# Row maxima recorded a step earlier in a two-layer attention kernel planned at build time

## The chip, the cores and the metric

The kernel runs on one core of one Trainium2 chip. The metric is the device time of one execution in microseconds (us), here 1409.2 us as the median of three runs (1408.99 to 1411.39). The profile is of one more execution, which took 1410.37 us.

## What is computed

Two conditioned attention layers over x of shape (8, 512, 512). The first is a linear attention with a softmax over the features of q and one over the tokens of k. The second, in which the change lies, is an ordinary softmax attention with 16 heads of 32 features in each of 8 batches:

```python
xn = layer_norm(x, norm_w, norm_b)
q = (xn @ q_w + q_b).reshape(Bx, Tx, H, -1)
k = (xn @ k_w + k_b).reshape(Bx, Tx, H, -1)
att = jnp.einsum('bnhl,bmhl->bnmh', q, k)
att = att + (1.0 - mask) * -1000000.0
att = jax.nn.softmax(att, axis=2)
v = ((xn @ v_w + v_b) * src_mask[:, :, None]).reshape(Bx, Tx, H, -1)
y = jnp.einsum('bnmh,bmhl->bnhl', att, v).reshape(Bx, Tx, Dx)
...
h = layer_norm(y, sb_norm_w, sb_norm_b) * (1.0 + scale) + shift
h = jax.nn.silu(h) @ out_w + out_b
return x + h
```

The softmax runs over the 512 keys of each query and head. Any number subtracted from all scores of one query and head drops out of it.

## The kernel before

**Recording and planning.** The kernel doesn't issue instructions as it is read. Every call (`nc.tensor.matmul`, `nc.sync.dma_start` and so on) is recorded by `Order`, with the tiles that it reads and writes; what depends on what follows from the order of recording (`touch`): a read that is recorded after a write waits for it, and a read recorded before a write makes that write wait. `Order.place` then makes a plan, twelve times over: an estimated duration for every instruction (`_takes`), an estimated time for every DMA (`DMA_ISSUE`, `DMA_LAND`, `DMA_RATE`), a list of what is ready for each engine, and of that the instruction with the earliest latest start (`slack`). The best of the twelve plans is issued, and each engine then runs its list strictly in that order. All instructions therefore carry line 476 in the profile, and are told apart by their tiles.

**The second layer** works in 32 groups G (8 batches b, 4 groups of 4 heads each, G = 4b + g). A group has two stacked operands in SBUF, `qst[G % 3]` and `kst[G % 3]`, of 106 rows, so three groups' stacks are alive at a time. Rows 0 to 97 hold q and k in two parts, and the mask. Rows 98 to 105 of `qst` hold the negated maximum of each query and head, in two parts; the same rows of `kst` select it, so that the product of all 106 rows is the score less that maximum.

- `l1_max(G)`: 16 products of 98 rows (queries on the partitions, 4 chunks by 4 heads), each followed by a maximum along the row on VectorE into `nm`. Then the maxima are split into `mi`, transposed by four small matmuls, copied to `aux` (tag `z`) on ScalarE, and a DMA on SyncE's queue spreads them into rows 98 to 105 of `qst` (lines 1089 to 1099).
- `l1_att(G)`: 16 products of 106 rows (keys on the partitions, key chunk m by head j), each followed by an exponential on ScalarE into a tile `e` (tag `A`), and after each key chunk `l1_av`, which multiplies by v and adds the exponentials up on GpSimd or VectorE.
- `l1_qk(G)`, `l1_stack(G)`: the projections of q and k, written out to DRAM and gathered from there into the stacks by six DMAs of 256 KB.
- `values`, `l1_y`, `l1_tail`, `transpose_x`: v, and the layer's output, interleaved by `pump` from a table of costs and due steps.

**The order of recording around the change.** `l1_max` and `l1_att` are generators. The loop at line 1422 records one of the 16 steps of `l1_att(G)` and then takes `next(maxes)` once, where `maxes` chains `l1_max(1)` to `l1_max(31)`; four `next` calls (`LEAD`) are made ahead of the loop, and in batch 7 group 28 makes eight more (lines 1424 to 1426). `l1_max(G)` has 15 yields between its 16 products, one ahead of `mi` (line 1088), and one at its end: 17 calls a group, of a loop that makes 16. So the `mi` part of group G is recorded in call 17 G, while the first score of group G is recorded after 4 + 16 G calls. Up to group 4 the maxima come first. From group 5 on the first G - 4 scores of a group are recorded ahead of the group's own maxima, and read the rows that the stack's previous user, group G - 3, left there; from group 20 on all 16 do. The loop makes 4 + 16 x 32 + 8 = 524 calls of the 527 that groups 1 to 31 ask for, so group 31 records 14 of its 16 maxima and no `mi` part.

Of the kernel before, what the change touches and what calls it, by code (L numbers as in the profile page):

```python
# [521 lines left out]
def kernel(ctx: ExitStack, tc: tile.TileContext, x, cond, mask0, mask1, w0, w1, out):  # L522
# [16 lines left out]
    def big(tag, name, dtype=F32, shape=(P, 512)):  # L539
        t = sb.tile(list(shape), dtype, name=name, tag=tag, bufs=BUFS[tag])  # L540
        if tag == "stk":
            nc.gpsimd.memset(t[:, :, 0:1].bitcast(F32), 0.0)
        return t

    def bank(tag, name, parts=P):
        tag = {"S": "mm", "ST": "mm", "a": "mm"}.get(tag, tag)
        return ps.tile([parts, 512], F32, name=name, tag=tag, bufs=BANKS[tag])
# [4 lines left out]
    def chunk(i):  # L552
        return slice(i * P, (i + 1) * P)
# [258 lines left out]
    st = {}  # L812
# [265 lines left out]
    def l1_max(G):  # L1078
        q, k = qst[G % 3], kst[G % 3]
        nm = sm.tile([P, NC, 4], F32, name=f"nm{G}", tag="nm4")  # L1080
        for c in range(NC):
            for j in range(4):
                if c or j:
                    yield
                sp = bank("S", f"s{G}{c}{j}")
                nc.tensor.matmul(sp, q[0:98, j, chunk(c)], k[0:98, j, :], start=True, stop=True)
                nc.vector.tensor_reduce(nm[:, c, j : j + 1], sp, AX.X, ALU.max, negate=True)
        yield
        mi = sm.tile([P, NC, 2, 4], F32R, name=f"mi{G}", tag="mi")
        nc.vector.tensor_copy(mi[:, :, 0, :], nm)  # L1090
        nc.vector.tensor_tensor(mi[:, :, 1, :], nm, mi[:, :, 0, :].bitcast(F32), ALU.subtract)
        mp = bank("S", f"mp{G}", 8)
        for c in range(NC):
            nc.tensor.transpose(mp[:, chunk(c)], mi[:, c].bitcast(F32).rearrange("p t j -> p (t j)"), ident)
        aux = big("z", f"aux{G}", shape=(8, 512))
        nc.scalar.copy(aux.bitcast(F32R), mp)
        nc.sync.dma_start(
            q[98:106].bitcast(F32), aux.unsqueeze(1).broadcast_to([8, 4, 512])
        )
        yield  # L1100

    SPARE = {(2, 2): "bWq", (2, 3): "bWk"}

    def l1_att(G):
        b, g = divmod(G, 4)
        q, k = qst[G % 3], kst[G % 3]
        if g == 0:
            st["yT", b] = []
        st["yp", G] = bank("a", f"yT{G}")
        st["acc", G] = []  # L1110
        for m in range(NC):
            cur = []
            for j in range(4):
                sp = bank("ST", f"t{G}{m}{j}")
                nc.tensor.matmul(sp, k[:, j, chunk(m)], q[:, j, :], start=True, stop=True)
                e = big(SPARE.get((m, j), "A"), f"e{G}{m}{j}")
                nc.scalar.activation(e, sp, AF.Exp)
                cur.append(e)
                if j == 1 and m > 0:
                    l1_av(G, m - 1)  # L1120
                yield
            st["e", G, m] = cur

    def l1_av(G, m):
        b, g = divmod(G, 4)
        while len(st["L1", "v", b]) <= m:
            st["need"]()
        es, yp = st.pop(("e", G, m)), st["yp", G]
        with order.together(845.0 if m or not G else 1690.0):
            if m == 0 and G > 0:  # L1130
                den = l1_den(G - 1)
            for j in range(4):
                h = 4 * g + j
                nc.tensor.matmul(
                    yp[32 * j : 32 * j + 32, :],
                    st["L1", "v", b][m][:, 32 * h : 32 * h + 32],
                    es[j],
                    start=(m == 0),
                    stop=(m == NC - 1),
                )  # L1140
        if m == 0 and G > 0:
            l1_den_keep(G - 1, den)
        acc = st["acc", G]
        if m == 0:
            acc.extend(es)
        else:
            for j in range(4):
                with order.on("gpsimd", "vector"):
                    nc.gpsimd.tensor_tensor(acc[j], acc[j], es[j], ALU.add)
        if m == NC - 1:  # L1150
            t = big("yT", f"yTs{G}")
            nc.scalar.copy(t, st.pop(("yp", G)))
            st["yT", b].append(t)
# [122 lines left out]
    for b in range(B + 1):  # L1276
# [5 lines left out]
        if b == 0:  # L1282
            bias_wide("L0", "Wv")
            run(first)
            split_w("L0", "Wv")
            bias_wide("L0", "Wq")
            split_w("L0", "Wq")
            prep_cond()
            with order.after(*st["L0", "xs", 1]):
                load_emb("L0", nc.sync)  # L1290
            l1_cols = load_cols("L1", list(COLS), nc.sync)
            run(second)
            run(l0_kn(b))
            split_w("L0", "Wo")
            load_bo("L0")
        else:
            run(mix(l0_y(b - 1), first, 4, 6))
            if last:
                l1_init(0)
                l1_stack(0)  # L1300
            run(islice(second, 26 if not last else 24))
            run(mix(hidden("L0", b - 1, "S"), second, 4, 7))
            tail = output("L0", b - 1, x[b - 1], x1[b - 1])
            if not last:
                run(mix(l0_kn(b), tail, 4, 12))
            else:
                load_x("L1", 1, x1[1])
                tail = mix(values("L1", 0), tail, 13, 12)
                run(mix(l1_max(0), tail, 1, 6))
# [56 lines left out]
    def ahead(b):  # L1366
# [5 lines left out]
        if n < B:  # L1372
# [5 lines left out]
            for g in range(3 if n else 4):  # L1378
                yield from l1_qk(4 * n + g)

    maxes = chain.from_iterable(l1_max(G) for G in range(1, NG))
    for _ in range(LEAD):
        next(maxes)
# [3 lines left out]
    for b in range(B):  # L1387
# [30 lines left out]
        for g in range(4):  # L1418
            G = 4 * b + g
            if G > 0:  # L1420
                l1_av(G - 1, NC - 1)
            for i, _ in enumerate(l1_att(G)):
                next(maxes, None)
                if b == B - 1 and g == 0 and i % 4 == 0:
                    for _ in range(2):
                        next(maxes, None)
                if i == STK and 0 < G < NG - 2:
                    while ("d", "Wq", G + 2) not in st:
                        need()
                    l1_stack(G + 2)  # L1430
                pump(16 * g + i)
# [60 lines left out]
```

## Time and profile before

| What | Value |
|---|---|
| Median of three runs | 1409.2 us |
| The profiled execution | 1410.37 us |
| Its span, first to last instruction | 1408.6 us |
| Mean granted TensorE clock | 0.992 |
| VectorE row maxima of the second layer | 510, mean 683 ns |
| Products of 98 rows | 510, mean 422 ns |
| Products of 106 rows | 512, mean 420 ns |
| DMAs `qst<-z` that spread the maxima | 31, 64 KB each |
| Idle time of PE in front of a matmul, by what ended it, ending with `DMA qst<-z` | 3.8 us, 2 times |

The page gives busy time by engine and by group of instructions. [...]matmuls overlap, and follow each other at about 235 ns in a run of products of 512 columns. An engine's name with a q is its queue. In a row of the waits, the engine and tile that waited stand left of the arrow, what ended the wait right of it, then the sum, the number and the longest. The chain of waits is the chain of work that ended last.

### The profile page before, as it was taken

The numbers are of one execution on the slowest core, as the hardware profiler recorded it, in microseconds if no ns is written. First come the engines' busy times: TensorE is split into PE (matmuls) and PEld (weight loads), VectorE is DVE, ScalarE is ACT, GpSimd is POOL, SyncE is SP. The second block draws the span as 40 slices with busy tenths as digits, with TensorE's granted clock in tenths as the row PEclk, the third lists the DMA queues.
The fourth block names the chain that finished last, engine by engine and source line by source line (L and its number), as shares of the span: only waits on it lengthen the run. The fifth ranks groups of instructions, "written<-read, shape, count | busy, mean of one in ns | idle before, by whom it ended". The sixth has DMA issues, their size and how long they took to land.

```text
span 1408.6 us, 20819 instructions
## 1 busy us (share of the span) xinstructions
PE 1370.6 (97%) x7385; PEld 956.9 (68%) x7385; DVE 1034.9 (73%) x1804; ACT 703.6 (50%) x1330; POOL 635.7 (45%) x721
## 2 busy tenths in 40 slices
PE   7999999999999998998999999999999999999996
PEld 4788878888888687556566566566666566666554
DVE  7665575666656568886878878778878777787987
ACT  4242323333234343654755655754854764764772
POOL 5123415133241312756537446555436546545661
PEclk9999999999999999999999999999999999999998
DMA  6413202021230456452553544544444535435311
GB/s 207 171 44 116 83 10 91 1 90 61 91 98 1 152 161 183 110 141 58 147 165 89 144 133 121 145 136 116 147 134 111 145 109 145 138 112 143 100 49 53
DMA packets 76397, 156.72 MB, mean 111 GB/s; under 512 B 8631, under 2 KB 8743, under 8 KB 76269
## 3 DMA queue, kind: packets, MB, share of 16 engines
q1 hardware_dynamic: 75952, 155.25, 37.8%
q8 instruction: 58, 0.95, 0.3%
q14 instruction: 47, 0.38, 0.1%
q0 software_dynamic: 288, 0.10, 0.0%
q10 hardware_dynamic: 52, 0.04, 0.0%
HBM read 102.86 MB, written 50.46 MB: 109 GB/s over the span
## 4 chain that ended last, share of the span: by engine, by line
PE 91%; DVE 5%; DMA 2%; ACT 1%; issue 1%; POOL 0%; SPq 0%; POOLq 0%; DVEq 0%; ACTq 0%
PE mm L476 91%; DVE nm L476 2%; DMA qst<-z 1%; DVE A L476 1%; DVE mi L476 1%; ACT mm L476 0%; DMA kst<-dWk 0%; DVE xc L476 0%; DVE y L476 0%; ACT y L476 0%; DMA xc<-in_x 0%; ACT A L476 0%; DVE mm L476 0%; DVE stb L476 0%; ACT h L476 0%
## 5 line engine op out<-in xcount | busy, mean ns | idle before, releaser
L476 POOL TENSOR_TENSOR A<-A,A 128x512 f32<-128x512 f32 x225 | 305.1, 1375 | 237.3 <-PE mm L476 139.3
L476 DVE TENSOR_REDUCE nm<-mm 128x1 f32<-128x512 f32 x510 | 335.2, 683 | 89.0 <-PE mm L476 86.0
L476 ACT ACTIVATE A<-mm 128x512 f32<-128x512 f32 x448 | 251.6, 602 | 161.1 <-PE mm L476 155.3
L476 PE MATMUL mm<-kst,qst 98*128 98x512 f32 x510 | 205.0, 422 | 4.6 <-DMA kst<-dWk 4.0
L476 PE MATMUL mm<-qst,kst 106*128 106x512 f32 x512 | 197.4, 420 | 5.3 <-DMA qst<-z 3.8
L476 PEld LDWEIGHTS mm<-kst,qst 98*128 98x128 f32 x510 | 97.8, 193 | 71.9 <-issue 33.5
L476 PE MATMUL mm<-A,v 128*32 128x512 f32 x896 | 138.5, 602 | 0.0
L476 POOL TENSOR_TENSOR y<-y,bo 128x512 f32<-128x512 f32 x60 | 79.5, 1327 | 128.2 <-DMA y<-in_x 82.6
L476 PEld LDWEIGHTS mm<-qst,kst 106*128 106x128 f32 x512 | 97.3, 193 | 58.6 <-issue 21.0
L476 PE MATMUL mm<-Wvh,xT 128*128 128x512 f32 x384 | 119.9, 414 | 0.0
L476 PE MATMUL mm<-xT,Wkh 128*128 128x512 f32 x384 | 116.9, 405 | 0.0
L476 DVE TENSOR_TENSOR A<-A,A 128x512 f32<-128x512 f32 x95 | 104.2, 1105 | 16.7 <-PE mm L476 8.8
L476 ACT ACTIVATE y<-mm,shL,scL 128x128 f32<-128x128 f32 (+1 forms) x144 | 76.4, 530 | 61.1 <-PE mm L476 57.7
L476 PE MATMUL mm<-ident,xc 128*128 128x128 f32 x512 | 88.1, 285 | 11.9 <-DVE xc L476 7.5
L476 PEld LDWEIGHTS mm<-ident,xc 128*128 128x128 f32 x512 | 64.5, 144 | 44.7 <-DVE xc L476 10.9
L476 PEld LDWEIGHTS mm<-Wvh,xT 128*128 128x128 f32 x384 | 71.0, 190 | 19.1 <-issue 2.8
L476 PEld LDWEIGHTS mm<-xT,Wkh 128*128 128x128 f32 x384 | 70.4, 189 | 18.7 <-ACT xT L476 2.3
L476 POOL TENSOR_SCALAR v<-bWv,cols 128x512 f32<-128x512 f32 x64 | 47.2, 747 | 73.1 <-PE mm L476 72.4
L476 ACT ACTIVATE mm<-mm,shL,scL 128x128 f32<-128x128 f32 (+2 forms) x152 | 76.0, 500 | 7.2 <-PE mm L476 7.0
L476 PE MATMUL mm<-xT,Wqh 128*128 128x512 f32 x256 | 75.5, 399 | 0.0
L476 POOL MEMSET bWk<- 64x4 f32 (+1 forms) x24 | 5.8, 243 | 147.3 <-PE mm L476 146.6
L476 ACT ACTIVATE hl<-mm,bcol 128x512 fp32r<-128x512 f32 x64 | 44.0, 687 | 56.3 <-PE mm L476 55.7
(221 smaller groups left out, 2675.1 us busy)
## 6 DMA issues: line engine op xcount, KB each, us to landing
kst<-dWk SPq DMA_DIRECT2D x96, 256.0 KB
qst<-dWq SPq DMA_DIRECT2D x96, 256.0 KB
dWk<-hl SPq DMA_DIRECT2D x32, 512.0 KB
dWq<-hl SPq DMA_DIRECT2D x32, 512.0 KB
xc<-in_x SPq DMA_DIRECT2D x32, 256.0 KB
y<-in_x SPq DMA_DIRECT2D x32, 256.0 KB
x<-y SPq DMA_DIRECT2D x32, 256.0 KB
xc<-x SPq DMA_DIRECT2D x32, 256.0 KB
```

The costliest lines, as they stand in the source:

```text
L476: getattr(engine, method)(*args, **kw)
```

## The change

The yield ahead of the `mi` part is taken out of `l1_max`, so that this part is recorded in the call that records the group's last product: 16 calls a group, as many as the loop makes. A mark `st["max"]` is set after it, and `l1_att` asserts when it is recorded that its group's maxima have been recorded. With this the `mi` part of group G is recorded in call 16 G, four calls ahead of the group's first score, for every group, and group 31 records all of its part.

```diff
@@ l1_max(G)
                 nc.tensor.matmul(sp, q[0:98, j, chunk(c)], k[0:98, j, :], start=True, stop=True)
                 nc.vector.tensor_reduce(nm[:, c, j : j + 1], sp, AX.X, ALU.max, negate=True)
-        yield
         mi = sm.tile([P, NC, 2, 4], F32R, name=f"mi{G}", tag="mi")
         nc.vector.tensor_copy(mi[:, :, 0, :], nm)
         nc.vector.tensor_tensor(mi[:, :, 1, :], nm, mi[:, :, 0, :].bitcast(F32), ALU.subtract)
...
         nc.sync.dma_start(
             q[98:106].bitcast(F32), aux.unsqueeze(1).broadcast_to([8, 4, 512])
         )
+        st["max"] = G
         yield
@@ l1_att(G)
         if g == 0:
             st["yT", b] = []
+        assert st["max"] >= G
         st["yp", G] = bank("a", f"yT{G}")
```

## The prediction

> **What bounds the kernel now.** I read the page first (engines, then the chain), then PE's waits, then the chain in time around the one long wait, then short stretches with the granted clock.
>
> ```profile
> PE 1370.6 (97%) x7385; PEld 956.9 (68%) x7385; DVE 1034.9 (73%) x1804; ACT 703.6 (50%) x1330; POOL 635.7 (45%) x721
> PE 91%; DVE 5%; DMA 2%; ACT 1%; issue 1%; POOL 0%; SPq 0%; POOLq 0%; DVEq 0%; ACTq 0%
> L476 DVE TENSOR_REDUCE nm<-mm 128x1 f32<-128x512 f32 x510 | 335.2, 683 | 89.0 <-PE mm L476 86.0
> L476 PE MATMUL mm<-kst,qst 98*128 98x512 f32 x510 | 205.0, 422 | 4.6 <-DMA kst<-dWk 4.0
> L476 PE MATMUL mm<-qst,kst 106*128 106x512 f32 x512 | 197.4, 420 | 5.3 <-DMA qst<-z 3.8
> ```
>
> PE is busy 97% of the span and makes 91% of the chain, so work added to PE is paid, and a wait at the head of PE's list is paid whole. The maxima are `mm<-kst,qst`, the scores `mm<-qst,kst`.
>
> ```profile
> PE mm L476 <- DVE xc L476: 7.5, 3, 5.9
> PE mm L476 <- DMA v<-in_mask_BxS_ff: 5.4, 1, 5.4
> PE mm L476 <- DMA kst<-dWk: 4.0, 1, 4.0
> PE mm L476 <- DMA qst<-z: 3.8, 2, 3.0
> ```
>
> These are PE's longest waits. Only the last is of the kind that the change multiplies: a score waits for its own group's maxima. The longer of its two is group 4's. In the chain:
>
> ```profile
> 614.39 20.81 PE mm L476 x111
> 635.22 0.58 ACT z L476
> 635.82 7.84 DMA qst<-z
> 643.80 18.62 PE mm L476 x97
> ...
> 902.81 4.96 DMA qst<-z
> ```
>
> The four transposes of `mi` start at 634.58 (PE's timeline), the copy to `z` ends and the DMA is issued at 635.82, 1.24 us later, and the scores start at 643.80. So this group needed 9.2 us from transposes to score, 7.84 of them for a 64 KB transfer. SyncE's queue tells why it took long: six stack transfers of 256 KB were issued between 631.92 and 634.8. The second wait (group 13, issue at 902.81, 4.96 us) cost 0.73 us. And the long one had a consequence:
>
> ```profile
> 640.00:644.00 4.00, 0.97 (x5) 0.52 (x4) 1.95 (x3) 0.00 (x0) 1.96 (x3) 1.00 0.68 100
> 644.00:648.00 4.00, 4.00 (x12) 3.13 (x12) 0.00 (x0) 3.05 (x6) 0.00 (x0) 0.57 0.01 3
> ```
>
> The columns are the stretch, its length, busy time of PE, PEld, DVE, ACT, POOL, then the granted clock: after PE idled for 3.03 us it ran at 0.57 of full clock in the next 4 us.
>
> **The change part by part.**
>
> *Work added.* Group 31 gets its last two products, two maxima, two small VectorE operations, four transposes, one ScalarE copy and one DMA. On PE: 2 x 0.235 us (start to start in PE's timeline) + 4 x 0.11 = **+0.9 us**, paid, for PE is the bound. VectorE's 2 x 0.683 + 2 x 0.18 = 1.7 us and ScalarE's 0.58 us lie beside PE's work (VectorE is busy about 40 of each 50 us here, ScalarE 30); uncovered they would cost just that. The mark and the assertion run while the kernel is recorded: nothing.
>
> *What becomes a wait.* Before, the scores wait for their own maxima in groups 0 to 4, in groups 5 to 19 from score number G - 4 on, and not at all from group 20 on; there the maxima are late work that nothing waits for. After it, the first score of all 32 groups waits, and behind it in PE's list stand the other scores, the v products, the projections: PE issues in order. So the question is how far ahead of the first waiting score the transposes stand, and how far they must.
>
> *How far they must.* I laid the built order of before against its trace, group by group. Before has 20 such waits. The time from transposes to the waiting score was 4.5 to 9.2 us; 18 of 20 cost PE nothing, among them gaps of 4.50, 4.52, 4.56, 4.68 and 4.85 us. So an ordinary group needs no more than 4.5. Below, I have 1.24 us plus a transfer: the nearest smaller row is the 4 KB DMA on GpSimd's queue, 1.9 us to landing, which gives 3.1. I take **4.2**, near the upper end since the gaps of 4.5 are of this very operation. Two in 20 needed more: 7.1 and 9.2, so 8.1 in one group of ten.
>
> *How far they stand after the change.* The built order of the changed program gives the instructions between transposes and first score. Counting 0.235 us for a product of 512 columns, 0.11 for a transpose and 0.24 for each product of the v and sum kind, and multiplying by 1.03 (with this count groups 1 to 4 of before come to 5.6, 6.6, 7.0, 6.1, against 5.82, 6.74, 7.20, 6.19 in the trace without the stall):
>
> | Groups | Gap, us | Stall: 0.9 x ordinary + 0.1 x long | Sum |
> |---|---|---|---|
> | 6, 14, 22, 31 | 3.4 to 4.1 | 0.9 x 0.3 + 0.1 x 4.2 | 2.8 |
> | 1, 8, 10, 12, 16, 18, 20, 24, 26, 28 | 4.7 to 5.0 | 0.1 x 3.2 | 3.2 |
> | 2, 3, 4 | 5.8 to 6.1 | 0.1 x 2.2 | 0.7 |
> | 5, 9, 13, 17, 21, 25 | 7.2 to 7.7 | 0.1 x 0.7 | 0.4 |
> | the other eight with larger gaps, and group 0 as before | 9.7 and more | 0 | 0 |
>
> That is 7.1 us, less the 3.8 that before pays: **+3.3 us**. The ends: if all ordinary needs are 3.1 and long ones don't occur, these stalls fall to 0, a gain of 3.8. If every group with a gap up to 5.0 needs 7.1, 14 x 2.3 = 32 us.
>
> *Two rules against the rows.* The Trainium skill, page "DMA: Bandwidth & Descriptors", section "Anatomy of one DMA — SWDGE (gpsimd) path", fits a transfer as about 2.0 us plus its bytes at 436 GB/s. For 64 KB that is an estimate of 2.15 us, so 3.4 us from transposes to score: hardly any group would stall and the change would cost 0.9 less the 3.8 it saves, a time of 1406. The rows say 7.84 and 4.96 for that transfer, on SyncE's queue with other transfers under way. I take the rows.
>
> The page "TensorE: Matmul & The Clock Gate", Part 1, says that an idle window of about 3.4 us halves TensorE's clock until a busy window has passed. This speaks against the change. The row agrees in kind: 3.03 us of waiting (with little work before) gave 0.57 over 4 us, a loss of 0.43 x 4 = 1.7 us, so a long stall costs 4.7 and not 3.0. Before has one such stall with this cause. With three or four long needs in 32 groups, half of them past 3 us, I count half a one more: **+0.9 us**. Were the rule's window not met by any, 0; were six met, 10.
>
> *The end.* From group 28 on before has maxima that lag behind the scores, up to 1370 us of the trace, and VectorE is busy with them:
>
> ```profile
> 1330.00:1340.00 10.00, 8.94 (x44) 4.17 (x43) 9.93 (x16) 7.23 (x16) 9.19 (x8) 1.00 0.49 129
> 1350.00:1360.00 10.00, 9.13 (x44) 4.78 (x43) 8.61 (x12) 8.09 (x19) 9.67 (x9) 1.00 0.07 26
> 1380.00:1390.00 10.00, 2.75 (x15) 2.02 (x14) 8.64 (x22) 1.73 (x4) 2.14 (x4) 0.74 0.07 27
> ```
>
> In the built order after the change, group 31's last maximum stands 16 us of PE work ahead of the last score, not 2. That frees VectorE at the end (PE lost 1.1 and 0.9 us in the first two rows), but the 16 last scores now come in a run of 10 us, against 16 x 0.602 = 9.6 us of exponentials on ScalarE alone. The third row, the wait on the last normalization, stays. Between -4 (these idles and some hidden ones) and +3: I take **0**.
>
> *Sum:* 0.9 + 3.3 + 0.9 + 0 = +5.1 us. The profiled execution, 1408.6 of span and 1.8 around it, becomes 1415.5; it stood 1.2 above the median of 1409.2, and with that offset taken off the forecast is **1414**.
>
> **Rivals.**
>
> *The queue decides* (chance 0.20). The stack transfers and the write-outs of 512 KB share SyncE's queue with `qst<-z`; the changed order puts write-outs or stack transfers directly ahead of it in most groups with gaps of 4.7 to 5.0. If half of the 14 tight groups need 7.1 or more: 7 x 2.3 = 16, with 0.9: 1426. For it: group 4's row. Against it: 18 of 20 waits of before cost nothing, under a mean DMA share near 0.45.
>
> *Cover is complete* (0.20). The need fits everywhere but in one or two groups, as now. Then only 0.9 is left and perhaps a microsecond: 1410.5. For it: between the first scores of groups 8 and 12, where every group still waits from its fourth to seventh following score on, before takes 108.5 us; between those of 20 and 24, where none waits, 108.7. Against it: the gaps of 3.4 to 4.1 are below any that the trace shows as free.
>
> *Faster by the end* (0.14). VectorE's late maxima are what holds the last 80 us: freed there, PE gains 5 us, and the two old waits of 3.8 go with the new order, against 0.9 and some 3.3 of small stalls: 4.6 less, 1404.6. It decides once the stalls of all groups stay under about 4 us in sum.
>
> The forecast's own case has 0.46.
>
> **How the numbers follow.** No change here means within 0.2%, 2.8 us, about what measurements of this kernel can tell. The forecast's case lies within 1412 to 1420 and is nearly always slower; of its 0.46 I give 0.44 to slower and 0.02 to same. The queue's 0.20 is slower. Cover is complete: 0.17 same, 0.03 slower. Faster by the end: 0.12 faster, 0.02 same. So 0.12, 0.21, 0.67. The range of 1404 to 1427 takes in both far cases down to two in ten outside, and the bounds of stalls and end.
>
> **What would show it.** After: 512 of both products, 32 `qst<-z`; PE's wait on `DMA qst<-z` at 6 to 9 us in 5 to 12 waits; one or two dips of clock more than before between 560 and 1380 us; the last `nm<-mm` at about 1360. It is wrong if that wait sums to 15 or more (the queue), or to under 4 with an unchanged time, or if the last score comes before 1372.9 us, where it comes now.

## The result, and the profile after

The changed kernel takes **1416.9 us** (median of five runs, 1415.49 to 1418.92) where the kernel before, run beside it, takes 1409.2. The ratio is 1.0052, with a 95% interval of 1.0037 to 1.0067: 5 to 9 us slower. The profiled execution took 1418.09 us, its span is 1416.3 us, and the granted clock is 0.992, as before. In what follows, "before" and "after" name the two kernels, and "half clock" a stretch in which the profile shows a granted clock of 0.5.

The page first, the same lines as were shown of before:

```profile
PE 1378.4 (97%) x7391; PEld 955.7 (67%) x7391; DVE 1044.8 (74%) x1802; ACT 707.0 (50%) x1331; POOL 637.5 (45%) x727
PE 91%; DVE 5%; ACT 2%; issue 1%; DMA 1%; POOL 0%; SPq 0%; ACTq 0%; DVEq 0%; POOLq 0%
L476 DVE TENSOR_REDUCE nm<-mm 128x1 f32<-128x512 f32 x512 | 333.7, 683 | 73.3 <-PE mm L476 69.8
L476 PE MATMUL mm<-kst,qst 98*128 98x512 f32 x512 | 205.1, 423 | 5.7 <-DMA kst<-dWk 4.0
L476 PE MATMUL mm<-qst,kst 106*128 106x512 f32 x512 | 197.6, 418 | 4.0 <-DVE y L476 2.2
```

The counts are as the change says: 512 products of both kinds. DMA's share of the chain went from 2% to 1%, and the last row shows why: the scores' worst wait is no longer the DMA that spreads the maxima but VectorE (`DVE y`). PE's waits say the same:

```profile
PE mm L476 <- DMA v<-in_mask_BxS_ff: 5.7, 1, 5.7
PE mm L476 <- DVE xc L476: 5.6, 2, 4.6
PE mm L476 <- DMA kst<-dWk: 4.0, 1, 4.0
PE mm L476 <- ACT A L476: 3.6, 7, 0.7
PE mm L476 <- DVE mi L476: 3.4, 8, 0.6
PE mm L476 <- ACT mm L476: 2.7, 9, 0.4
PE mm L476 <- DVE y L476: 2.6, 2, 2.2
...
PE mm L476 <- DMA qst<-z: 0.9, 1, 0.9
```

The wait that all 32 groups now have fell from 3.8 us to 0.9, and it is one wait, of group 31. No row of the list has grown by more than 3.0 us (`ACT A`, from 0.6).

**Where the 7.7 us of span are.** Since PE is the bound, I compare the two traces at points where PE has done equal work. Work is counted from the first product of the second layer, 0.235 us for a product of 512 columns and smaller values for the others; other values for the smaller ones move the bounds by up to 0.7 us. The first stage ends where before stands at 658.6 us, behind group 4's wait, and the second where it stands at 1276.0.

| Stage | Before, us | After, us | Difference |
|---|---|---|---|
| Start to group 4 and its wait | 658.6 | 655.0 | -3.6 |
| Middle, groups 4 to 27 | 617.4 | 622.1 | +4.7 |
| End, with all added work | 132.6 | 139.3 | +6.7 |

In the first stage the wait of 3.03 us and the half clock behind it are gone. That gain is given back in the middle and then lost once more at the end.

**The end.** Stretches of after: busy time of PE, PEld, DVE, ACT and POOL, then granted clock, DMA share and GB/s:

```profile
1340.00:1350.00 10.00, 8.34 (x40) 4.07 (x39) 8.28 (x12) 7.73 (x17) 8.77 (x11) 1.00 0.75 170
...
1360.00:1370.00 10.00, 8.61 (x39) 3.93 (x38) 5.38 (x7) 8.09 (x19) 8.81 (x8) 0.83 0.22 60
1370.00:1380.00 10.00, 7.76 (x43) 3.61 (x41) 7.40 (x7) 8.35 (x19) 7.00 (x5) 0.97 0.19 54
```

The last two rows of the same stretches in before:

```profile
1360.00:1370.00 10.00, 9.98 (x57) 5.59 (x56) 8.54 (x16) 6.40 (x14) 5.96 (x5) 1.00 0.31 86
1370.00:1380.00 10.00, 9.81 (x57) 5.17 (x57) 9.59 (x14) 4.85 (x11) 5.86 (x6) 1.00 0.28 82
```

Before has 57 matmuls in each and idles for 0.02 and 0.19 us. After has 39 and 43, idles for 1.4 and 2.2 us, and has the clock halved for part of each row. PE's timeline of after has the places (start, length, what, idle before it):

```profile
1363.64 0.90 PE L476 MATMUL mm<-qst,kst 106*128 106x512 f32 x2 [0.93 <-DMA qst<-z]
1365.01 1.12 PE L476 MATMUL mm<-Woh,h 128*128 128x512 f32 x3 [0.46 <-ACT h L476]
...
1379.41 0.80 PE L476 MATMUL mm<-qst,kst 106*128 106x512 f32 x1 [2.24 <-DVE y L476]
```

The last line is the last score of all. What ended its wait is `y<-y,mm` on VectorE, which reads a PSUM bank (`mm`) that the score is to write, and VectorE's timeline shows what that stood behind, GpSimd's what ran beside it:

```profile
1373.01 0.69 DVE L476 TENSOR_TENSOR A<-A,A 128x512 f32<-128x512 f32 x1
1373.98 3.11 DVE L476 TENSOR_TENSOR A<-A,A 128x512 f32<-128x512 f32 x2 [0.28 <-ACT A L476]
1377.01 1.75 DVE L476 TENSOR_TENSOR A<-A,bWq 128x512 f32<-128x512 f32 x1
1378.68 0.67 DVE L476 TENSOR_TENSOR y<-y,mm 128x512 f32<-128x512 f32 x1
...
1373.00 5.21 POOL L476 TENSOR_TENSOR A<-A,A 128x512 f32<-128x512 f32 x3 [4.19 <-PE mm L476]
1378.17 1.71 POOL L476 TENSOR_TENSOR A<-A,bWk 128x512 f32<-128x512 f32 x1
```

The additions of exponentials stand ahead of it in VectorE's list. The first took 0.69 us, the next three 1.43, 1.76 and 1.75. Of these only the first waited for ScalarE (0.28 us); all three run beside additions on GpSimd, and each ends 0.55 us behind the end of one. Before has group 31's maxima as other work between these scores (PE's last product of them starts at 1370.1 us); after starts its last at 1355.7.

### The profile page after: what moved, and what is told of

It is laid out like the page before. It is cut to its first block, busy times and chain, and to the rows that moved or that the text cites. A ratio compares the mean times of both kernels' runs of the same rounds, so it can differ in the third digit from the quotient of the medians.

```text
span 1416.3 us, 20877 instructions
## 1 busy us (share of the span) xinstructions
PE 1378.4 (97%) x7391; PEld 955.7 (67%) x7391; DVE 1044.8 (74%) x1802; ACT 707.0 (50%) x1331; POOL 637.5 (45%) x727
## 4 chain that ended last, share of the span: by engine, by line
PE 91%; DVE 5%; ACT 2%; issue 1%; DMA 1%; POOL 0%; SPq 0%; ACTq 0%; DVEq 0%; POOLq 0%
PE mm L476 91%; DVE nm L476 1%; DVE mi L476 1%; DVE A L476 1%; ACT mm L476 1%; ACT y L476 1%; ACT A L476 1%; DMA kst<-dWk 0%; DVE y L476 0%; DMA rawL0Wk<-in_L_cond_Wk 0%; DVE xc L476 0%; DMA out<-y 0%; DVE mm L476 0%; DVE hl L476 0%; DVE stb L476 0%
## 5 line engine op out<-in xcount | busy, mean ns | idle before, releaser
L476 POOL TENSOR_TENSOR A<-A,A 128x512 f32<-128x512 f32 x235 | 318.6, 1378 | 233.1 <-PE mm L476 148.2
L476 ACT ACTIVATE A<-mm 128x512 f32<-128x512 f32 x448 | 254.6, 602 | 141.7 <-PE mm L476 131.1
L476 PE MATMUL mm<-A,v 128*32 128x512 f32 x896 | 144.0, 607 | 0.9 <-ACT A L476 0.7
L476 DVE TENSOR_TENSOR A<-A,A 128x512 f32<-128x512 f32 x85 | 86.9, 1035 | 9.7 <-PE mm L476 8.6
L476 DVE SCALAR_TENSOR_TENSOR hl<-mm,bcol,hl 128x512 fp32r<-128x512 f32 x64 | 47.7, 745 | 33.4 <-ACT hl L476 33.4
```

What stands on the lines that cost most here:

```text
L476: getattr(engine, method)(*args, **kw)
```

## Experiments

Times are medians; the ratio is against the kernel before, run on the same chip. "Stages" are the three of the table above.

**1. The added work alone.** Before, with what group 31 lacks recorded at the end.

```diff
+    for _ in maxes:
+        pass
     l1_av(NG - 1, NC - 1)
```

> Before, with what is left of the maxima of group 31 (two products, two row maxima, the mi part) recorded behind the last scores: the added work alone, with no score waiting for it and nearly the same order on PE. If the added work is all but free (waits, order or the last groups cost the 7.7 us), the time is within 1409 to 1411, ratio 1.000 to 1.001. If the added work at the end itself is what costs, 1413 or more.

1413.04 us against 1410.42, ratio 1.0016 (1.0008 to 1.0025): the added work costs 1 to 3.5 us. So it isn't all but free: the time stands where the second case of the expectation begins. Stages 655.9, 617.7 and 133.9: the end grew by 1.3, in a profiled execution that, at 1409.29, was the fastest of twelve. Group 4's wait in this execution was 1.92 us with no half clock behind it, though its order is that of before up to there, so 2.7 us of the first stage differ between executions of one order.

**2. The wait taken away, planned anew.** The maxima go to DRAM, the scores' rows are constant (so the scores are not shifted), and the planner sees this.

```diff
...
-        nc.sync.dma_start(q[98:106].bitcast(F32), aux.unsqueeze(1).broadcast_to([8, 4, 512]))
+        zd = dr.tile([8, 4, 512], F32, name=f"zd{G}")
+        nc.sync.dma_start(zd, aux.unsqueeze(1).broadcast_to([8, 4, 512]))
```

> After, but the maxima are written to DRAM instead of into the q stack, whose rows 98 to 105 hold a constant 1: all of the work of after, recorded in its order, and no score waits for a maximum. If the wait of the scores is what costs, the time falls back to about 1410 (ratio 1.000 to 1.001). If the order of recording alone costs (maxima in step with the scores, 16 calls a group), it stays at 1415 to 1418 (ratio 1.004 to 1.006). If the wait costs only at the end (group 31), about 1412.

1434.24 us, ratio 1.0156 (1.0134 to 1.0177), far from what any theory gave. PE's waits show that the test was not clean:

```profile
PE mm L476 <- DVE mi L476: 16.0, 13, 2.8
```

With no reader behind it, the `mi` part has no time by which it is due. The planner put the four transposes where PE had to wait for VectorE. It says nothing of the DMA wait, but it shows a second place in the chain where PE can be made to wait: ahead of the transposes.

**3. Without the eight extra calls of group 28**, which served the old count of 17.

```diff
-                if b == B - 1 and g == 0 and i % 4 == 0:
-                    for _ in range(2):
-                        next(maxes, None)
```

> After without the eight extra calls in group 28, which no longer have a lag to make up; the order up to group 28 is that of after. If the loss sits in the last groups because the extra calls push the maxima of 29 to 31 ahead and bunch the last scores, this gains 2 to 5 us (1412 to 1415). If the loss sits in the long middle or in the wait itself, it stays within 1 us of 1417, or gets worse by 2 where group 31 then waits longer.

1415.99 us, ratio 1.0041 (1.0028 to 1.0054). Stages 655.5, 621.2, 137.7. The waits of the last scores are gone (0.42 us of idle in the last 16, against 3.62 in after), and there is no half clock among them, yet the end is only 1.6 us shorter and still 5.1 longer than in before; this plan stalls 2.06 us for `mi` at 1342.8. The extra calls aren't the main cause, and the waits between the last scores are the form that the loss takes in after, not a necessary one.

**4. Another plan of before.** A constant of the planner's estimate, `WEIGHTS`, moved by one.

```diff
-WEIGHTS = 110.0
+WEIGHTS = 111.0
```

> Before with one number of the planner's estimates moved by under one per cent (WEIGHTS 110 to 111), which makes another plan out of the same recorded program. If plans scatter by only a microsecond or two, 1408 to 1411 and the 7.7 us are the change's own. If plan scatter explains the difference, it comes out 4 us or more away from 1409.2, either way.

1411.89 us, ratio 1.0010 (1.0002 to 1.0019). The same work in a slightly different plan is 0 to 3 us slower.

**5. The wait taken away, the order kept.** Experiment 2 done cleanly: the plan is made for the changed kernel, and only when it is issued do the 32 DMAs go to DRAM. All engines have after's order. The scores are again not shifted.

```diff
...
+    for o, to in swap:
+        method, args, kw = o.calls[0]
+        o.calls = [(method, (to, *args[1:]), kw)]
```

> After with its plan untouched: the same instructions in the same order on every engine, but when the plan is issued the 32 DMAs of the maxima go to DRAM and the rows 98 to 105 of the q stack hold a constant 1. So nothing but the wait itself is taken away. If the waits cost what the prediction put on them (about 7 us of stalls in 32 groups, and half clock behind the long ones), the time falls to 1409 to 1411. If the order costs and the waits are met in time (after's trace shows 0.9 us of them), it stays within 1.5 us of after, 1415 to 1417, ratio 1.004 to 1.005.

1417.33 us, ratio 1.0047 (1.0034 to 1.0060), the same as after. PE's waits no longer list `qst<-z`, but the wait of the last score stands where it stood:

```profile
1378.84 0.79 PE L476 MATMUL mm<-qst,kst 106*128 106x512 f32 x1 [2.25 <-DVE y L476]
```

Group 31's wait of 0.93 us is gone too, and the time did not move. So **the scores' wait for the DMA that spreads the maxima costs the changed kernel nothing that can be measured; the loss lies in the order in which it now does things**, and in the other waits of that order, such as those for `mi` at the transposes, which this run keeps. The run decides against the main term of the forecast.

**6. The end of before on the changed kernel.** Group 28 makes no calls, so that in groups 29 to 31 the scores stand ahead of the maxima again; the assertion is left out.

```diff
...
-                next(maxes, None)
-                if b == B - 1 and g == 0 and i % 4 == 0:
-                    for _ in range(2):
-                        next(maxes, None)
+                if G != NG - 4:
+                    next(maxes, None)
```

> After up to group 28, but group 28 makes no calls for maxima, so that groups 29 to 31 have their scores ahead of their own maxima as in before, interleaved to the end (their scores read the rows of the stack's previous user). If the loss sits in the last three groups, whose maxima now come first and whose scores are then bunched, this recovers 5 to 6 us of the 7.7: 1410 to 1412. If it sits in the long middle, it stays at 1415 or more.

1422.51 us, ratio 1.0089 (1.0076 to 1.0102): worse, against expectation. Stages 655.0, 622.0, 144.0. Sixteen calls left out at once leave too much for the last groups: the last score comes at 1387.9 us instead of 1379.4. Late maxima are no help in themselves.

**7. The end of after on before.** The converse: before up to group 27, then group 28 makes calls enough to catch up.

```diff
-                if b == B - 1 and g == 0 and i % 4 == 0:
+                if b == B - 1 and g == 0:
```

> Before up to group 27 with its lag, then 32 extra calls in group 28 catch up, so that groups 29 to 31 have their maxima ahead of their scores as in after. The mirror of the run with the end of before. If the last three groups cost, 1414 to 1416 although the middle is before's. If the middle costs, 1409 to 1411.

1418.13 us, ratio 1.0058 (1.0046 to 1.0070), more than either case expected. Stages 658.2, 617.5, 142.7: start and middle are those of before to within 0.4 us, and the end alone loses 10.1 us. Part of the loss is waits in the catching up:

```profile
1307.97 0.50 PE L476 MATMUL mm<-kst,qst 98*128 98x512 f32 x1 [0.71 <-DVE nm L476]
1309.18 1.22 PE L476 MATMUL mm<-qst,kst 106*128 106x512 f32 x2 [0.71 <-DMA qst<-z]
```

Behind these PE ran at half clock for 6.8 us. With 6 the reading is narrow: the end is sensitive to its order, and two ways of rearranging it cost 5 and 10 us.

**8. Another plan of after.** The planner's estimate of a transfer's landing, `DMA_LAND`, at 2410 instead of 2400.

```diff
-DMA_ISSUE, DMA_LAND, DMA_RATE = 560.0, 2400.0, 260.0
+DMA_ISSUE, DMA_LAND, DMA_RATE = 560.0, 2410.0, 260.0
```

> After with one of the planner's estimates moved by under one per cent (DMA_LAND 2400 to 2410): another plan of the same recorded program. If the 7.7 us are the change's own, it stays within 2 us of 1417. If after's plan was an unlucky draw, it comes out at 1413 or less.

1413.25 us, ratio 1.0022 (1.0014 to 1.0031): half of the loss is gone with a nudge, to just above what was named for an unlucky plan. Stages 651.3, 621.3, 136.8. The middle is nearly as long as in after; 3.7 of the 6.8 us that its profiled span is shorter by lie in the first stage, where the half clock at 559 us lasted 3.4 us and not 6.8. It was 3.4 us long in experiment 1 as well, in before's order, so this part isn't the plan's. The profiled execution, at 1411.28, was one of the fastest of this kernel (1410.96 to 1415.23), and after's was above its median.

**9. More distance.** The changed kernel without the extra calls, with `LEAD` at 8.

```diff
-    LEAD, STK = 4, 7
+    LEAD, STK = 8, 7
...
```

> The changed kernel without group 28's eight extra calls, and with the maxima eight calls ahead of the scores instead of four, so that every group's copy of the maxima stands some eight products further ahead of its first score. Theory of the end (what counts is that nothing is left to lie between the last scores): the longer lead makes the last run of scores without maxima longer, not shorter, so no gain, 1415 to 1422. Rival (the scores stand too close behind their maxima): 1408 to 1412, better than the changed kernel without the extra calls at 1416.0.

1417.64 us, ratio 1.0052 (1.0039 to 1.0064). Stages 656.9, 623.5, 136.9. More distance behind the maxima brings nothing, as experiment 5 said it should not. It brought a new wait: PE now reaches the next group's products before their stack does (`DMA qst<-dWq`, 6.6 us in 6 waits).

**10. The repair done the other way.** The yield stays, and the loop makes the seventeenth call itself, at each group's last score. No extra calls in group 28; the assertion is left out. The group's maxima stand ahead of its scores as they do in after.

```diff
+        yield
         mi = sm.tile([P, NC, 2, 4], F32R, name=f"mi{G}", tag="mi")
...
-                if b == B - 1 and g == 0 and i % 4 == 0:
-                    for _ in range(2):
-                        next(maxes, None)
+                if i == 15:
+                    next(maxes, None)
```

> The yield stays, the loop makes a seventeenth call at the last score of each group, and group 28 makes no extra ones: the maxima keep their four calls of lead, and the part behind them still stands in a call of its own. The same maxima stand ahead of the same scores as in the changed kernel. Theory (order and the end): slower than before by 0.2 to 0.6%, 1413 to 1418. Rival (the changed kernel only drew a bad plan): 1408 to 1412.

**1411.56 us, ratio 1.0005 (0.9997 to 1.0013)**: not told from before. My theory gave 1413 to 1418; the number of the rival, a bad plan, holds. Stages 658.3, 617.9, 134.4: middle and end as before, but for the added work, and a first stage without the gain that after has there. And PE waits more often for the maxima here than in any kernel of the plain change:

```profile
PE mm L476 <- DVE mi L476: 6.2, 14, 1.4
...
PE mm L476 <- DMA qst<-z: 3.2, 6, 0.7
```

A typical one:

```profile
801.82 0.60 PE L476 MATMUL mm<-ident,mi 128*8 128x128 f32 x4 [0.32 <-DVE mi L476]
...
806.54 0.70 PE L476 MATMUL mm<-qst,kst 106*128 106x512 f32 x2 [0.51 <-DMA qst<-z]
```

From transposes to score it is 4.72 us, of which PE waited 0.51.

**11. and 12. More plans.** `DMA_LAND` at 2410 on before, and at 2390 on after.

> The kernel before with the planner's estimate of a transfer's landing at 2410 instead of 2400, the same nudge that brought the changed kernel from 1416.9 to 1413.3: another plan of the same work. If plans scatter by two to four us for either kernel and the change itself costs some 4 to 6 us, this stays within 1407 to 1413. If the nudge helps whatever it is put to, 1405 to 1407. If before's plan was a lucky one, 1412 to 1416, and the change has no cost of its own.

> The changed kernel with the planner's landing estimate at 2390 instead of 2400: a third plan of the changed kernel. If the change has a cost of its own beside the scatter of plans: 1412 to 1419, with the waits between the last scores and a half clock there again. If its cost is one unlucky plan: 1408 to 1411.

Before: 1410.37 us, ratio 1.0001 (0.9992 to 1.0011). After: 1417.00 us, ratio 1.0045 (1.0031 to 1.0059), stages 655.8, 620.9, 137.7, with the wait of 2.25 us ahead of the last score again. The half clock among the last scores that was expected with it did not come.

**What the plans say together:**

| Order | Times, us | Middle | End |
|---|---|---|---|
| before (before, 4, 11) | 1409.2, 1411.9, 1410.4 | 617.4 to 619.9 | 132.3 to 132.9 |
| `mi` in the last product's call, lead of four (after, 3, 8, 12) | 1416.9, 1416.0, 1413.3, 1417.0 | 620.9 to 622.1 | 136.8 to 139.3 |
| the same, lead of eight (9) | 1417.6 | 623.5 | 136.9 |
| `mi` in a call of its own (10) | 1411.6 | 617.9 | 134.4 |

Kernels of one order lie 2.7 to 3.7 us apart, and the loss is larger than that. But the nudges made few new plans. With the tiles of PE's list compared place by place in the traces, 11 differs from before in 21 of 7385 places, and 4 in 129, all in the middle. Of after's 7391 places, 8 differs in 45, 12 in 834, none of them at the end, and 3 in 362, all at the end. So the change has two distinct plans of the middle (after, 12) and two of the end (after, 3), and 9 is a third order of its kind. All of them are longer in both stages than before's plans and 10. That the loss is the change's own, and not that of unlucky plans, is likely by this and not shown.

**Where the middle loses.** I counted the time around PE's transposes of `mi` beyond that of their number, from the start before to the start behind each run of them: 1.2 us in before, 5.9 in after, 5.0 in experiment 8, 3.5 in 12. In after that is +4.7, the size of the middle's difference. The reason for these waits is on VectorE. Its two `mi` operations in the middle, in before (minimum, median and maximum in ns):

```profile
L476 DVE CAST mi<-nm x22: 141/176/1328, 667.2 to 1267.0; 128x16 fp32r<-128x16 f32 x22
L476 DVE TENSOR_TENSOR mi<-nm,mi x22: 174/176/1221, 667.4 to 1267.3; 128x16 fp32r<-128x16 f32 x22
```

and in after:

```profile
L476 DVE CAST mi<-nm x22: 174/978/1319, 685.3 to 1264.3; 128x16 fp32r<-128x16 f32 x22
L476 DVE TENSOR_TENSOR mi<-nm,mi x22: 175/1206/1221, 686.6 to 1265.3; 128x16 fp32r<-128x16 f32 x22
```

The same 128 x 16 elements take a median of 176 ns in before and 978 and 1206 in after. Over the whole trace after has 53 `mi` operations of more than 0.3 us; all 53 overlap a GpSimd operation and end 0.03 to 0.04 us behind the end of one. Most of their time is waiting for GpSimd. In before the `mi` part falls mostly into pauses of GpSimd's additions (29 of 62 operations are long), in after mostly beside them (53 of 64), so the maxima reach PE some 1.8 us later. The planner reckons with 630 ns for each of the two (`_takes`), so in after the input of the transposes is often not ready when their place in the list comes. The trace names `mi` for only part of it (2.0 us of PE's waits in before, 3.4 in after). But the size alone does not settle it. Experiment 10 has its `mi` operations held as long:

```profile
L476 DVE CAST mi<-nm x23: 174/920/1228, 661.1 to 1263.5; 128x16 fp32r<-128x16 f32 x23
L476 DVE TENSOR_TENSOR mi<-nm,mi x23: 176/1181/1222, 662.3 to 1264.5; 128x16 fp32r<-128x16 f32 x23
```

It has 4.1 us around the transposes of `mi` and no loss in the middle; around those of `xc` it has 7.4, against 9.8 in before. Experiment 9 has about 5 and 4 us around the two, less in sum than before, and the longest middle of all. So that GpSimd holds the `mi` part back and PE waits for it is shown; that this is what makes the middle longer is not. No run took this wait away, and the cause of the middle's loss stays open.

## Why the prediction was right and wrong

The sign and the size were right: 1414 was forecast, 1416.9 measured, slower by 7.7 us of span where the sum gave +5.1. **The mechanism was wrong, and that the number came out is luck.** Of the sum, 4.2 us did not come, and 3.6 were gained in the first stage; what makes up for it are the middle and the end, which it set to nothing.

*Work added, +0.9.* Experiment 1 measured 1 to 3.5 us for it, recorded at the end, and experiment 10's last stage is 1.8 longer than before's. Right in kind, rather too small; how much of the rest is VectorE's and ScalarE's 2.3 us, which were put beside PE's work, was not measured.

*What becomes a wait, +3.3.* This is the step that failed. Measured: 0.9 us in one wait, against 3.8 before, so -2.9; and without any such wait the time is the same (experiment 5). Its terms were off. The gaps "3.4 to 4.1" were counted from the built order; the trace has 4.54, 4.60 and 4.52 us for groups 6, 14 and 22, which did not stall, and 4.59 for group 31, of which 0.93 are the wait. The count takes every instruction at full speed, and in the first three PE took longer. The long needs of 7.1 and 9.2, taken as one group in ten, did not come at all. And the ordinary need of 4.2 was too small: group 31 needed 4.59, and four groups of experiment 10 have gaps of 4.69 to 4.72 with 0.47 to 0.51 of waiting in them, so the order left some 4.2 and 4.7 was needed. Groups 6, 14 and 22 had nothing to spare.

*The two rules.* I had taken the rows of 7.84 and 4.96 us for the 64 KB transfer against the page's fit of 2.0 us plus bytes, which the page gives for transfers issued by GpSimd, and these are SyncE's. In after there was one stall in 32, as the fit's side had it, but the size lies between: needs of 4.6 to 4.7, less the 1.24 ahead of the issue, leave about 3.4 us for the transfer, where the fit's estimate was 2.15. The two long rows had six and five large transfers issued on the queue in the 5 us ahead of them. In after no spread has more than four, and those with four (groups 0, 7, 11, 15, 19, 23 and 27) had 8.6 us or more, so a long need there would not have shown. Of the clock rule the sum made +0.9. The half-clock stretches of the two traces sum to the same 23.9 us: group 4's of 3.4 and the one at 794.2 are gone, and two of 3.4 stand in the last scores. So this term was 0.

*The end, 0, between -4 and +3.* Measured +6.7, with the added work in it. The prediction saw the pieces (16 us of work ahead of the last score instead of 2, and the last 16 scores closer together) and took VectorE's freedom as a gain of the same size. It isn't free there: in the last scores additions of exponentials take the maxima's place in its list, up to 1.76 us apiece beside GpSimd's, and the last score stands behind three of these. The last 16 scores, forecast in a run of 10 us, took 15.8. (1.7 us come back at the wait on the last normalization, 5.89 and 1.36 us in PE's timeline of before, 4.56 and 1.02 in after.)

*What no step had.* The middle, +4.7. "Cover is complete" argued that groups that wait and groups that don't take the same time (108.5 and 108.7 us), and this was sound for the DMA. The part of the chain ahead of it, from the last maximum over `mi` to the transposes, was costed as 2 x 0.18 us of VectorE work for group 31 alone; in after its two medians add up to 2.2 us, and PE waits at the transposes. How much of the 4.7 this makes is open.

*The signs named.* 512 products and 32 spreading DMAs came; more dips of the clock did not (two between 600 and 1380 us in either trace). The wait at 6 to 9 us didn't; it fell under 4, and the time did change, so neither of the two tests written down fits: the list of signs lacked a loss with no long wait. The last maximum came at 1356.1 us, forecast 1360.

*The rivals.* "The queue decides" and "Faster by the end" didn't come. "Cover is complete" was right about the waits and wrong about the time. That its 1410.5 can be had with the maxima in order is shown by experiment 10, at 1411.56.

**What stays open.** Besides the cause of the middle's loss: experiment 10 is one plan, and it was not planned again with a constant moved; whether a call of its own for the `mi` part is better as such, or this plan was a good one, isn't settled. Between before and it no difference can be measured, so no version beat before.

## What to carry to other kernels

When a repair turns late work into work with a deadline, follow the whole chain up to that deadline and not only its last link: here the DMA at its end was covered, while PE came to wait for two small VectorE operations ahead of it, and the last scores lost the late work that had stood between them. To tell a wait from the order that comes with it, keep the planned order and take the dependence out at issue; taking it out ahead of the planner measured another plan. Where a planner decides the order, plan each side several times before a difference of a few us is called the change's, and compare the plans: here kernels of nearly one order lay up to 3.7 us apart, and moving a constant changed as few as 21 of PE's 7385 places.

## What the hardware showed that was not expected

Small VectorE operations that start while a GpSimd operation runs are held until that ends: 174 ns became up to 1.3 us, and all 53 such ends in after lie 0.03 to 0.04 us behind a GpSimd end. The additions `A<-A,A` on VectorE show the same: 0.68 us for the 10 in after with no GpSimd operation beside them, a median of 0.98 for the 75 with one, and the 44 of more than 0.8 us all end 0.55 us behind a GpSimd end. The row maxima, which read PSUM, do not: the 310 with a GpSimd operation beside them have a median of 682 ns and none is over 694, the other 202 a median of 683. The Trainium skill, page "SBUF — State Buffer", section "Who interferes with whom", describes it: an addition with two inputs in SBUF, or a cast in a two-port mode, and a GpSimd instruction that reads SBUF take one port pair in turn, whole instructions at a time. The trace agrees, down to the end times. The row that would have told this was in the profile of before, as the maximum of 1328 ns beside a median of 176.

Half clock came in pieces of 3.4 us (3.4, 6.8 or 10.2 long) in all traces, and what a wait costs depends on more than its length. Group 4's wait in the one order of before was followed by 3.4 us of it at a wait of 3.03 us and by none at 1.92, and in the plan of experiment 11 by 6.8 at 2.63. The wait of 2.24 or 2.25 us ahead of the last score, in one order of PE's list, was followed by 3.4 us in after, by 6.8 in experiment 5 and by none in 12.
